# Four edits to a two-layer transformer kernel: loads of the FFN's first token rows, preset rows of a table, unread products in TensorE's waits, and the place of the last shared expert

## The chip, the cores and the metric

The kernel runs on one core of one Trainium2 chip, in fp32. The metric is the device time in microseconds of one execution. The kernel before takes 2078.44 us, the median of three runs (2077.82, 2078.44, 2081.33). TensorE is called PE, VectorE DVE, ScalarE ACT, GpSimd POOL and SyncE SP.

## The reference

The input `x` has 8 batches of 512 tokens with 256 channels. Four residual blocks follow one another; each normalises `x` first.

```python
x = x + _L0_attn_ref(_layernorm(x), ...)  # 16 heads, relative positions in 128 buckets, own layernorm
x = x + _L0_ffn_ref(_layernorm(x), ...)
x = x + _L1_attn_ref(_layernorm(x), ...)
x = x + _L1_ffn_ref(_layernorm(x), ...)
```

In the second block (shortened below) each batch has weights of its own: token rows 1 to 16 of the batch are split into even and odd ones, and their outer products are added to the common weights.

```python
lt = x[:, 1:17, :]; even = lt[:, ::2, :]; odd = lt[:, 1::2, :]
m1 = (even[:, :4, :, None] * odd[:, :4, None, :]).reshape(Bx, Hx, Dx)
m2 = (even[:, 4:, :, None] * odd[:, 4:, None, :]).reshape(Bx, Dx, Hx)
h = einsum('bsd,hd->bsh', x, W1) + scale * einsum('bsd,bhd->bsh', x, m1) + b1
out = einsum('bso', gelu(h), W2) + scale * einsum(gelu(h), m2) + b2
```

The third block is attention over the batch dimension, with a mask under which the first four batches see batches 0 to 3 only, and the last four see all eight. The fourth is a mixture of 32 experts. A token takes 4 of them, chosen out of its 2 best groups of 8 by sigmoid scores, and adds the output of a shared expert, which every token passes through.

## The kernel before

The first block (`_l0_attention`, from 0 to about 1081 us) runs over a list of attention steps. A dictionary (`prefetch`, L585 on) says which pieces of the next block's preparation are done how many steps before its end: at -12 the load of w1T, at -8, -6, -5 and -4 batch 0's statistics, its normalised tile `xn0` and its two transposes, and at the last step the load of w2T.

The second block (`_FFN`, 1082 to about 1325 us) runs over the 8 batches. For one batch, `hidden` (L676) makes 8 tiles of 128 hidden channels, each of two products 128x128 by 128x512 accumulated in PSUM tile `ph`; `output` (L684) makes four output tiles; `fold` (L641 for w1b, L646 for w2b) makes the next batch's own weights on DVE, eight operations on each. The even rows that `fold` multiplies must stand on all 128 partitions. `norm` writes 16 token rows to a small table in DRAM (L609), and `spread` (L614) loads 8 of them back into `even`, 128 partitions x 8 x 256, 1 MB in one DMA. For batch 0 that load is issued when the FFN begins; for the others it is issued at f = 2 of the batch before. All these DMAs are on SP's queue.

On that queue, too, `fill` (L693) writes zeros into one eighth of `rows`, the table of 160 x 128 rows in DRAM through which routed tokens reach their experts: at f = 2 of batches 0 to 6 for the first seven parts, and after the last output of batch 7 for the last one. The last call then writes a column of numbers from tile `spare` (L697, 20480 elements of 4 bytes).

The third block and the routing of the fourth (`_l1`, 1325 to about 1810 us) run over 8 units u of 512 tokens. Their order is written out by hand: `at(time, f)` puts a call on a list, `hop` puts a call in two halves on it, and the list is sorted by time and emitted in that order on all engines. Each unit's chain is `multiplied` (DVE, prod), `summed` (PE, ps, L972), `scored` (PE, pts, L988; ACT copies sc), `softmax1` and `softmax2` (DVE and ACT), then per seen batch `weighted` (DVE, value) and `gathered` (PE, ao, L1025, eight transposes accumulated in PSUM), and `projected` (PE, po). `prepare` transposes and projects a unit that comes two later (PE pq, pv; L935, L947). PSUM tiles come from the two-buffer pool `quick`, among others.

A unit is routed one unit later, interleaved with the next unit's attention: `norm2` (ACT, xn), `turn2` (PE, pt, L1088), `logits` (PE), `hidden` twice (PE pg and pu, ACT act; the shared expert's two halves, L1248), `route` (DVE, sfc to tmp to sel), `count`, `take` and `send` (PE pc, pb, pk and DVE between), `gated` twice (DVE, hid), `copied` four times (ACT, pay), `add_shared` (PE pos). Then POOL scatters the unit's 16 groups of rows to the table by indirect DMAs (L879). `pace` issues two of these at a time, and each pair waits for what DVE did last at that point. The last unit's routing stands alone, since no attention comes after it; this part is called the rear here.

`experts` reads off which expert owns each of the 160 tiles. Then the expert stage (1816 to 2090 us) fetches tile after tile of the table (r, L1414, on SP, each waiting for the last 16 scatters), transposes it (PE ptr, L1432; rT), multiplies (pge, L1440), transposes and multiplies again (pth, poe), and scatters results.

Of the kernel before, what the change touches and what calls it, by code (L numbers as in the profile page):

```python
# [21 lines left out]
P = 128  # L22
# [532 lines left out]
class _FFN:  # L555
# [30 lines left out]
    def prefetch(self):  # L586

        return {
            -200: [self.constants],
            -12: [self.load],  # L590
            -8: [partial(self.measure, 0)],
            -6: [partial(self.norm, 0)],
            -5: [partial(self.turn, 0, 0)],
            -4: [partial(self.turn, 0, 1)],
            0: [self.load2],
        }

# [5 lines left out]
    def norm(self, b, bank, pool):  # L603
        nc = self.nc
        xn = self.xn[b] = (pool if b else self.carry).tile([P, NT, H], F32, tag="xn" if b else "xn0", name="xn")
        for t in range(NT):
            _normalize(nc, xn[:, t, :], self.x[b][:, t, :], *self.stats[b], t)
            if t == 0:
                nc.sync.dma_start(self.token_rows[b % 2], xn[1:17, 0, :])  # L609

    def spread(self, b, pool):

        even = pool.tile([P, 8, H], F32, tag="even", name="even")
        self.nc.sync.dma_start(  # L614
            even, self.token_rows[b % 2].rearrange("(i two) c -> two i c", two=2)[0].partition_broadcast(P)
        )
        w1 = pool.tile([P, NK, FF], F32, tag="w1b", name="w1b")
        w2 = pool.tile([P, NF, H], F32, tag="w2b", name="w2b")
        self.w[b] = even, w1, w2
# [14 lines left out]
    def fold(self, b, n):  # L634

        nc = self.nc
        even, w1, w2 = self.w[b]
        for i in range(4):
            if n < 2:
                cols = slice(i * H, (i + 1) * H)  # L640
                nc.vector.scalar_tensor_tensor(  # L641
                    w1[:, n, cols], even[:, i, :], self.odd[:, n, i : i + 1], self.w1[:, n, cols], ALU.mult, ALU.add
                )
            else:
                view = lambda w: w.rearrange("p (r q) o -> p q r o", q=2)[:, n - 2, :, i * 64 : (i + 1) * 64]
                nc.vector.scalar_tensor_tensor(  # L646
                    view(w2),
                    even[:, 4 + i, :].rearrange("p (o r) -> p r o", r=4),
                    self.odd[:, n - 2, 4 + i : 5 + i],
                    view(self.w2),  # L650
                    ALU.mult,
                    ALU.add,
                )

    def run(self, rest, after):

        nc, tc, x, rows = self.nc, self.tc, self.x, self.rows
        with ExitStack() as ctx:
# [30 lines left out]
            def fill(n):  # L689

                part = slice(n * NS // B, (n + 1) * NS // B)
                to = rows.rearrange("(s p) c -> p s c", p=P)[:, part]
                filled.append(nc.sync.dma_start(to, empty.unsqueeze(1).to_broadcast([P, NS // B, ROW])))  # L693
                if n == B - 1:
                    with nc.allow_non_contiguous_dma(reason="a column of rows"):
                        filled.append(
                            nc.sync.dma_start(  # L697
                                rows.rearrange("(s p) c -> p s c", p=P)[:, :, H : H + 1].bitcast(I32), spare.unsqueeze(2)
                            )
                        )  # L700

            with tc.manual_schedule():
                self.spread(0, sb)
                nc.gpsimd.memset(empty, 0.0)
                nc.sync.dma_start(spare, self.a["spare"])
                for n in range(4):
                    self.fold(0, n)
                for b in range(B):
                    hT = sb.tile([P, NF, S], F32, tag="hT", name="hT")
                    for f in range(NF):  # L710
                        hidden(b, f)
                        if rest:
                            rest.pop(0)(bank, sb)
                        if f == 1:
                            for t in range(NT):
                                nc.gpsimd.tensor_tensor(x[b][:, t, :], x[b][:, t, :], self.b2, ALU.add)
                        if b == B - 1:
                            if f == 2:
                                after.measure(0)
                            elif f == 3:  # L720
                                after.shift(0)
                            elif f == 4:
                                after.norm(0)
                            continue
                        if f == 0:
                            self.measure(b + 1, bank, sb)
                        elif f == 2:
                            self.norm(b + 1, bank, sb)
                            self.spread(b + 1, sb)
                            fill(b)  # L730
                        elif f in (4, 5):
                            self.turn(b + 1, f - 4, bank, sb)
                    for t in range(NT):
                        output(b, t)
                        if b + 1 < B:
                            self.fold(b + 1, t)
                    if b == B - 1:
                        fill(b)
                    elif b == 2:
                        after.load()  # L740
        return filled

# [59 lines left out]
def _l1(nc, tc, a, x, out, ident, mhalf, rows, results, filled, inputs, early):  # L802
# [14 lines left out]
    with ExitStack() as ctx:  # L817
# [72 lines left out]

        waiting = deque()

        def pace():

            for _ in range(min(2, len(waiting))):
                after(waiting.popleft()(), [vec.last] if vec.last is not None else [])

        def quick(name):

            return ps_a.tile([P, S], F32, tag="psa", name=name)  # L900
# [401 lines left out]
        def at(time, f, *args):  # L1302
            events.append((time, len(events), partial(f, *args)))
# [26 lines left out]
        def attend(u, t):  # L1330
# [10 lines left out]
            )  # L1341
            at(t + when[0], softmax1, u)
            at(t + when[1], softmax2, u)
            for m in range(n):
                at(t + when[2][m], weighted, u, m)
                at(t + when[2][m] + 1.4, gathered, u, m)
# [3 lines left out]
        def routed(u, t, n):  # L1350

            at(t + 0.2, measure2, u)
            at(t + 5.0, norm2, u)
            at(t + 8.2, turn2, u)
            at(t + 10.0, logits, u)
            at(t + 13.4, hidden, u, 0)
            at(t + 20.0, hidden, u, 1)
            split = route(u)
            at(t + 15.3, next, split)
            at(t + (21.1 if n == 8 else 19.0), next, split, None)  # L1360
            late = 3.5 if n == 8 else 0.0
            hop(count, u, first=t + 23.4 + late / 2, then=t + 25.0 + late)
            at(t + (19.6 if n == 8 else 18.9), gated, u, 0)
            hop(take, u, first=t + 26.0 + late, then=t + 27.8 + late)
            at(t + 29.5 + late, gated, u, 1)
            for i in range(TOPK):
                at(t + 24.6 + late + 1.1 * i, copied, u, i)
            hop(send, u, first=t + 28.0 + late, then=t + 30.5 + late * 1.8)
            for r in range(2):
                hop(add_shared, u, r, first=t + 32.6 + late + r, then=t + 36.5 + late * 2 + 0.7 * r)  # L1370
            for i in range(8):
                at(t + 36.0 + late * 1.8 + 2.6 * i, pace)

        T = [40.0 if seen(u) == 4 else 48.0 for u in range(U)]
        start = [sum(T[:u]) for u in range(U + 1)]
        at(-29.0, biases)
# [22 lines left out]
        with tc.manual_schedule():  # L1399
            for _, _, f in events:  # L1400
                f()
            while waiting:
                pace()
            experts()
        routing.close()
        tp = pool("m_t", 2)
        ps_r = pool("m_psr", 2, space=PSUM)
# [277 lines left out]
```

## Time and profile before

| what | value |
|---|---|
| timed runs, median (lowest, highest) | 2078.44 us (2077.82, 2081.33) |
| the profiled execution, whole | 2102.91 us |
| its span | 2101.1 us |
| its mean granted TensorE clock | 0.954 |
| PE busy | 1930.6 us, 92% |
| PE weight loads (beside it) | 1334.9 us, 64% |
| DVE, ACT, POOL busy | 1389.0, 1106.3, 1143.3 us |
| chain that ended last | PE 63%, DVE 11%, DMA 11%, issue 5%, POOL 5%, ACT 3% |
| DMA moved | 444.43 MB, 212 GB/s mean |

By stage, PE is busy as follows, with the mean granted clock and the DMA engines' share:

| stretch, us | what | PE busy, us | clock | DMA |
|---|---|---|---|---|
| 1026 to 1082 | end of the first block | 49.37 of 56 | 0.94 | 0.75 |
| 1082 to 1325 | FFN | 234.34 of 243 | 0.99 | 0.60 |
| 1325 to 1794 | units and routing | 385.40 of 469 | 0.90 | 0.18 |
| 1794 to 1816.5 | wait for routed rows | 0.00 of 22.5 | 0.50 | 0.35 |
| 1816.5 to 2090 | experts | 268.39 of 273.5 | 0.99 | 0.73 |

The profile is of one execution, so durations are read from it and the times to compare from the runs. In a line of a timeline the columns are start, duration, engine, line of code, operation, output tile and inputs with their shapes, and the number of instructions put together; what stands in brackets at the end is how long the engine was idle before it and what ended that. A waits row gives engine and line, what it waited for, total us, number of waits and longest wait.

### The profile page before, as it was taken

Reading aid. Unit: us, or ns where it says so; the run is one execution under the profiler, and the core shown is the slowest. Engines: PE = TensorE matmul, PEld = TensorE weight load, DVE = VectorE, ACT = ScalarE, POOL = GpSimd, SP = SyncE. Lnnn points to the kernel's source line nnn. Section 1 sums busy time; section 2 is a strip of 40 time slices with the busy share of each in tenths; the row PEclk is TensorE's granted clock in tenths of the full one; section 3 lists DMA queues with packets and bytes.
Section 4 is the critical chain, followed back from the end, with each engine's and each line's share of the span. In section 5 each row is a group of like instructions: output and inputs, shape, how many; then the busy total and the mean of one; then the engine's idle time right before and its main releaser. Section 6 shows DMA issues by size and latency. Waiting matters only on the chain.

```text
span 2101.1 us, 49496 instructions
## 1 busy us (share of the span) xinstructions
PE 1930.6 (92%) x17956; PEld 1334.9 (64%) x17956; DVE 1389.0 (66%) x3731; ACT 1106.3 (53%) x2366; POOL 1143.3 (54%) x1340
## 2 busy tenths in 40 slices
PE   7999999999999999999889999879888778599997
PEld 4666667666666666676656666545455455388786
DVE  3677777777777777777676454257876775356666
ACT  2677777767777777677631222345433422144443
POOL 4666777767778686776733111114444443455555
PEclk7999999999999999999989999999989987699999
DMA  8999999999999999899944548601111115457888
GB/s 270 305 317 284 310 303 300 292 289 304 295 297 304 296 306 299 286 289 299 285 140 143 167 141 127 20 1 42 42 42 42 42 42 215 169 163 217 256 254 266
DMA packets 388928, 444.43 MB, mean 212 GB/s; under 512 B 43344, under 2 KB 367952, under 8 KB 388688
## 3 DMA queue, kind: packets, MB, share of 16 engines
q1 hardware_dynamic: 373904, 401.93, 63.9%
q0 software_dynamic: 13824, 38.29, 5.0%
q8 instruction: 145, 2.38, 0.5%
q10 hardware_dynamic: 960, 1.05, 0.1%
q14 instruction: 95, 0.78, 0.1%
HBM read 238.99 MB, written 202.19 MB: 210 GB/s over the span
## 4 chain that ended last, share of the span: by engine, by line
PE 63%; DVE 11%; DMA 11%; issue 5%; POOL 5%; ACT 3%; SPq 1%; another core or an unknown queue 0%; POOLq 0%; DVEq 0%; ACTq 0%
PE sc L372 7%; PE sc L384 6%; PE pge L1440 6%; PE et_ps L412 5%; PE po L684 5%; DMA winp<-shift 5%; PE ctx_ps L424 5%; PE pq L291 5%; PE ph L676 3%; PE poe L1458 3%; PE pa L315 3%; DMA shift<-strip 3%; PE pq L935 2%; PE po L460 2%; DVE prod L796 2%
## 5 line engine op out<-in xcount | busy, mean ns | idle before, releaser
L398 DVE CUSTOM_DVE_ANT_0 e<-sc,winc 128x512 f32<-128x512 f32 x512 | 333.3, 689 | 268.1 <-PE sc L384 139.4
L401 ACT ACTIVATE e<-e,low 128x512 f32<-128x512 f32 x512 | 365.7, 715 | 94.8 <-DVE low L398 93.5
L322 ACT COPY strip<-pa 128x512 f32<-128x512 f32 x512 | 275.2, 591 | 138.6 <-POOL winc L352 58.2
L325 POOL TENSOR_TENSOR own<-aside,strip 128x512 f32<-128x512 f32 x256 | 269.1, 1051 | 130.3 <-ACT strip L322 121.6
L415 DVE COPY et<-et_ps 128x512 f32<-128x512 f32 x512 | 328.5, 683 | 0.7 <-PE et_ps L412 0.7
L372 PE MATMUL sc<-sm,sm 32*128 32x256 f32 (+3 forms) x1792 | 310.5, 437 | 0.2
L315 PE MATMUL pa<-pos,sm 32*128 32x256 f32 x2048 | 297.2, 407 | 1.7 <-ACT sm L299 1.0
L879 POOL DMA_INDIRECT rows<-pay,slot x128 | 141.4, 1105 | 237.2 <-issue 224.9
L352 POOL TENSOR_TENSOR winp<-winp,own 128x256 f32<-128x256 f32 x256 | 187.3, 732 | 108.0 <-DMA winp<-shift 78.3
L372 PEld LDWEIGHTS sc<-sm,sm 32*128 32x128 f32 x1792 | 164.1, 184 | 97.0 <-DVE et L415 35.6
L384 PE MATMUL sc<-ident,winp 128*128 128x128 f32 x1280 | 204.9, 287 | 22.4 <-DMA winp<-shift 21.1
L879 POOL DMA_INDIRECT results<-y,r x160 | 157.0, 981 | 124.3 <-ACT y L1460 70.7
L352 POOL TENSOR_TENSOR winc<-winc,own 128x256 f32<-128x256 f32 x256 | 187.2, 731 | 52.2 <-DMA winc<-shift 40.6
L384 PEld LDWEIGHTS sc<-ident,winp 128*128 128x128 f32 x1280 | 137.4, 142 | 102.0 <-issue 58.3
L315 PEld LDWEIGHTS pa<-pos,sm 32*128 32x128 f32 x2048 | 178.5, 187 | 11.5 <-issue 2.0
L412 PE MATMUL et_ps<-ident,e 64*128 64x64 f32 x4096 | 184.2, 230 | 1.1 <-DVE et L415 1.1
L58 POOL TENSOR_TENSOR rstd<-var,mhalf 128x2 f32<-128x2 f32 (+1 forms) x56 | 51.1, 912 | 241.5 <-DVE var L56 208.9
L412 PEld LDWEIGHTS et_ps<-ident,e 64*128 64x128 f32 x4096 | 148.9, 140 | 44.4 <-issue 22.8
L1440 PE MATMUL pge<-store,rT 128*128 x640 | 168.0, 385 | 3.5 <-DVE rT L1434 1.1
L424 PE MATMUL ctx_ps<-et,v 128*32 128x128 f32 x4096 | 166.6, 281 | 0.5 <-DVE et L415 0.5
L291 PE MATMUL pq<-xnT,wqk 128*128 128x512 f32 x256 | 134.0, 646 | 0.1
L679 ACT ACTIVATE hT<-ph,b 128x512 f32<-128x512 f32 x64 | 44.0, 687 | 165.6 <-PE ph L676 165.5
(216 smaller groups left out, 3339.0 us busy)
## 6 DMA issues: line engine op xcount, KB each, us to landing
shift<-strip SPq DMA_DIRECT2D x256, 510.0 KB
winp<-shift SPq DMA_DIRECT2D x128, 384.0 KB
winc<-shift SPq DMA_DIRECT2D x128, 384.0 KB
winp<-shift SPq DMA_DIRECT2D x128, 256.0 KB
winc<-shift SPq DMA_DIRECT2D x128, 256.0 KB
rows<-empty SPq DMA_DIRECT2D x8, 2640.0 KB
r<-rows SPq DMA_DIRECT2D x160, 132.0 KB
z<-results SPq DMA_DIRECT2D x32, 512.0 KB
```

Of the source, the lines that this page charges most:

```text
L315: nc.tensor.matmul(pa[:, t * W : (t + 1) * W], src[rs, i * P : (i + 1) * P], pos[rs, g, :], start=True, stop=True)
L322: nc.scalar.copy(st[:, 2 * j : 2 * j + 2, :].rearrange("p t w -> p (t w)"), pas[j])
L352: nc.gpsimd.tensor_tensor(dst, dst, own[:, t], ALU.add)
L372: nc.tensor.matmul(sc[:, c0:c1], s[side_][rs, cut : cut + P], s[2 + side_][rs, c0:c1], start=c0 == 0, stop=False, skip_group_check=True,)
L384: nc.tensor.matmul(sc[:, m * P : (m + 1) * P], wins[n + 2 * (m - i)][1][:, j, (i - m + 1) * P : (i - m + 2) * P], ident, start=False, stop ...
L398: nc.vector.tensor_tensor_reduce(e, sc, wins[n][0][:, j, :], 1.0, -LOW, ALU.add, ALU.min, low)
L401: nc.scalar.activation(e, e, AF.Exp, bias=low, scale=-1.0, accum_out=totals[b, g // 2][:, i, r : r + 1])
L412: nc.tensor.transpose(bank[:, c : c + 64], e[rs, m * P : (m + 1) * P], ident[rs, rs])
L415: nc.vector.tensor_copy(et[:, f].rearrange("p j m q -> p (j m q)"), bank)
L424: nc.tensor.matmul(ctx_ps[32 * r : 32 * r + 32, i * P : (i + 1) * P], vs[b % 2][:, m, g % 2, g // 2 * 4 + r, :], et[:, :, m, :], start=m = ...
L879: ins = nc.gpsimd.indirect_dma_start(to, bass.IndirectOffsetOnAxis(ap=index, axis=0), source, None, bounds_check=last)
L1440: nc.tensor.matmul(pg[:, :H], rT[:, k * P : (k + 1) * P], w[:, k * H : (k + 1) * H], start=k == 0, stop=k == NK - 1)
```

## The change

There are four parts.

1. Batch 0's first four even rows are loaded at step -3 of the first block, into a tile that takes over a slot of the carried pool ("xn2"). For every batch the tile `even` becomes two tiles of half the size, loaded by one DMA each; `fold` of w1b reads the first, of w2b the second.
2. The last `fill` is called at f = 7 of the last batch but one, not after the last output; the column of numbers is written by a call of its own at f = 0 of the last batch.
3. `busy(n)` issues n products of 128x128 by 128x512 on weights that lie in SBUF, into a PSUM tile that nothing reads. They are put at times before the first `gathered` of units 0, 1, 4, 5, 6 and 7, before a `summed` or `gathered` of units 6 and 7, and at 8.19 after the beginning of the last routing; 14 more, in pairs, stand behind seven of the last 13 scatters, each pair waiting for one of them.
4. In the rear, the shared expert's second `hidden` and both `gated` come at 30.9 to 31.5, behind both halves of `send` (28.0 and 30.5), not at 18.9 to 29.5; the 16 scatters of the last unit no longer wait for DVE's last operation.

```diff
+            -3: [self.spread_first],
...
+    def even_rows(self, b, half, pool, tag):
+        even = pool.tile([P, 4, H], F32, tag=tag, name="even")
+        rows = self.token_rows[b % 2].rearrange("(i two) c -> two i c", two=2)[0]
+        self.nc.sync.dma_start(even, rows[4 * half : 4 * half + 4].partition_broadcast(P))
+        return even
+
+    def spread_first(self, *_):
+        self.first = self.even_rows(0, 0, self.carry, "xn2")
...
-        even = pool.tile([P, 8, H], F32, tag="even", name="even")
-        self.nc.sync.dma_start(
-            even, self.token_rows[b % 2].rearrange("(i two) c -> two i c", two=2)[0].partition_broadcast(P)
-        )
+        even = [self.even_rows(b, 0, pool, "even0") if b else self.first, self.even_rows(b, 1, pool, "even1")]
...
-                    w1[:, n, cols], even[:, i, :], self.odd[:, n, i : i + 1], self.w1[:, n, cols], ALU.mult, ALU.add
+                    w1[:, n, cols], even[0][:, i, :], self.odd[:, n, i : i + 1], self.w1[:, n, cols], ALU.mult, ALU.add
...
-                    even[:, 4 + i, :].rearrange("p (o r) -> p r o", r=4),
+                    even[1][:, i, :].rearrange("p (o r) -> p r o", r=4),
...
                         if b == B - 1:
-                            if f == 2:
+                            if f == 0:
+                                number()
+                            elif f == 2:
...
+                        elif f == 7 and b == B - 2:
+                            fill(b + 1)
...
-                    if b == B - 1:
-                        fill(b)
-                    elif b == 2:
+                    if b == 2:
...
-        def pace():
+        def pace(free=False):
             for _ in range(min(2, len(waiting))):
-                after(waiting.popleft()(), [vec.last] if vec.last is not None else [])
+                ins = waiting.popleft()()
+                if not free:
+                    after(ins, [vec.last])
+
+        def busy(n, behind=()):
+            idle = quick("idle")
+            for _ in range(n):
+                ins = nc.tensor.matmul(idle, inputs.wqkv[:, 0, :P], inputs.wqkv[:, 1, :S], start=True, stop=True)
+                if behind:
+                    after(ins, behind)
+                    behind = ()
...
+            if u in WAITS:
+                at(t + when[2][0] + 1.39, busy, WAITS[u])
+            if u >= U - 2:
+                at(t + 7.89, busy, 3)
...
+            if u + 1 == U:
+                at(t + 8.19, busy, 4)
...
-            at(t + 20.0, hidden, u, 1)
+            rear = u + 1 == U
+            at(t + (31.0 if rear else 20.0), hidden, u, 1)
...
-            at(t + (19.6 if n == 8 else 18.9), gated, u, 0)
+            at(t + (30.9 if rear else 19.6 if n == 8 else 18.9), gated, u, 0)
...
-            at(t + 29.5 + late, gated, u, 1)
+            at(t + (31.5 if rear else 29.5 + late), gated, u, 1)
...
-                at(t + 36.0 + late * 1.8 + 2.6 * i, pace)
+                at(t + 36.0 + late * 1.8 + 2.6 * i, pace, u + 1 == U)
+        WAITS = {0: 5, 1: 2, 4: 5, 5: 1, 6: 3, 7: 3}
...
             experts()
+            for ins in scattered["rows"][-13::2]:
+                busy(2, [ins])
```

More of the change, by code (lines that the diff above doesn't have):

```diff
@@ L693, in fill, with number @@
                 filled.append(nc.sync.dma_start(to, empty.unsqueeze(1).to_broadcast([P, NS // B, ROW])))
[L694 to L699, printed above, removed]
+            def number():
+                with nc.allow_non_contiguous_dma(reason="a column of rows"):
+                    filled.append(
+                        nc.sync.dma_start(
+                            rows.rearrange("(s p) c -> p s c", p=P)[:, :, H : H + 1].bitcast(I32), spare.unsqueeze(2)
                         )
+                    )
             with tc.manual_schedule():
```

## The prediction

> **What bounds the kernel.** I read the page's engine totals and its strip of slices first, then the chain, then TensorE's waits, then windows of 3.41 us. TensorE (PE) is busy 1930.6 of 2101.1 us and carries 63% of the chain, so the end moves with PE time or with what PE waits for.
>
> ```profile
> PE   7999999999999999999889999879888778599997
> PEclk7999999999999999999989999999989987699999
> ```
>
> Each digit of these rows is 52.5 us. After the first slice the granted clock is lowered in slice 20 (1051 to 1103 us, where the FFN begins) and in slices 29 and 32 to 34 (1523 to 1576 and 1681 to 1839 us, units 4 to 7 and the rear). Those stretches are where the change works. PE's waits from 1325 to 1830 us (total, count, longest) say why:
>
> ```profile
> PE ao L1025 <- DVE value L796: 32.2, 10, 7.1
> PE ptr L1432 <- DMA r<-rows: 23.1, 1, 23.1
> PE ps L972 <- DVE prod L796: 9.5, 7, 4.3
> ...
> PE pt L1088 <- ACT xn L1076: 5.4, 1, 5.4
> ```
>
> A wait is dear twice: itself, and at the clock behind it. The granted clock moves only on a grid of 3.41 us. Columns: stretch, its length, busy PE, PEld, DVE, ACT, POOL, granted clock, DMA share, GB/s.
>
> ```profile
> 1369.04:1372.46 3.42, 0.00 (x0) 0.00 (x0) 1.20 (x3) 2.09 (x3) 0.00 (x0) 0.50 0.01 2
> 1410.00:1413.41 3.41, 1.43 (x10) 1.19 (x11) 3.27 (x21) 0.90 (x2) 0.00 (x0) 1.00 0.01 2
> 1519.23:1522.64 3.41, 1.54 (x5) 0.47 (x4) 3.13 (x17) 3.33 (x5) 0.00 (x0) 1.00 0.00 0
> 1737.68:1741.09 3.41, 3.41 (x17) 3.01 (x15) 3.38 (x10) 0.00 (x0) 0.00 (x0) 0.50 0.00 0
> ```
>
> The reader sees the idle slot at half clock; a slot 42% busy that kept it (next slot full); one 45% busy after which it fell; and a slot filled wholly with transposes and narrow products that did not raise it. Over all slots, at most 0.40 busy always dropped and 0.48 or more never.
>
> **First rows of the FFN (5.2 us).** Before, the 1 MB of even rows is issued at 1081.92, when the FFN begins; folds start at 1087.64 and PE's first hidden product follows.
>
> ```profile
> 1087.64 3.26 DVE L641 SCALAR_TENSOR_TENSOR w1b<-even,odd,w 128x256 f32<-128x256 f32 x8 [5.00 <-DMA spare<-in_spare]
> ...
> 1088.23 3.75 PE L676 MATMUL ph<-xnT,w1b 128*128 128x512 f32 x4 [6.39 <-issue]
> ```
>
> Afterwards batch 0's first half lands three attention steps earlier. The fold starts at about 1081.9, the cn multiply (0.69) and seven folds of 0.41 follow, and PE's two k halves run at about 1082.4 and 1084.7. The first hidden tile is done at about 1085.5, not 1091.65: 6.1 earlier. But DVE, which still folds w2b (4.74) and then normalises batch 1, moves only from 1095.56 to about 1090.6, and batch 1's transposes queue on PE behind that normalising. I take 5.2; 4 if the second half, still issued at 1081.9, comes late to the w2b folds, 6.5 if DVE has slack. On SP the early half stands before the w2T load, which comes 0.5 to 1.5 us later and is wanted only at 1085.9: nothing. Every batch has two half loads in place of one, one SP issue of 0.41 us more each, in an SP queue whose wait is for DMA: nothing, at most 0.4 in all.
>
> **Last preset and number column (0).** In the instruction order of the built programs the last two fills, the numbers and the next loads stand on SP in the same order with equivalent waits as before. SP already runs ahead:
>
> ```profile
> 1277.42 7.94 SPq L693 DMA_DIRECT2D rows<-empty  x2
> 1299.70 0.36 SPq L697 DMA_DIRECT2D rows<-spare  x1
> ```
>
> The first line's start follows batch 7's token rows (written at 1275.60), the numbers follow the landing of the last fill, and ACT's first xlT copy, which waits until they land at about 1333.7, keeps PE waiting 6.8 us. All of it moves with the FFN and none of it with the new places: 0, and the FFN's 5.2 carries through.
>
> **Products in the waits.** One 128x128 by 128x512 product is half of a two-product tile: 0.86 us at full clock, 1.71 at half (pg, four products in 3.41 to 3.62 us). Their own waits are on ACT reads long finished; whatever is queued behind them on PE was waiting for DVE anyway. They cost nothing if they are shorter than the wait and save only what is now run slowly behind it.
>
> Unit 0: five products (4.27) in 7.08 us. The slow work behind, ao 1.97 instead of 1.09 and pq 5.08 instead of 3.44, is 2.5. A hole of 2.8 remains, which can straddle a grid line; I take half, 1.25 (0.8 to 2.5). Unit 1: no drop here, 0 (to 1.5 in other executions). Unit 4: five in 6.78 leave 2.5, at most 1.9 behind; 1.4. Unit 5: one product in 1.52, while the 4.25-us wait later (for tmp) stays: 0. Unit 6: three before ps 0.4, and three in front of the first ao:
>
> ```profile
> 1680.18 1.97 PE L1025 MATMUL ao<-ident,value 128*128 128x128 f32 x8 [4.21 <-DVE value L796]
> ...
> 1689.09 1.23 DVE L796 TENSOR_TENSOR value<-v,sc 128x1024 f32<-128x1024 f32 x1 [2.62 <-PE ao L1025]
> ```
>
> DVE there waits 2.62 for the slow ao's to free a value buffer; at full clock that wait goes: 2.6, with ps 3.0. Unit 7 has the same 4.21 and the same 2.62 at 1744.00: 2.6. Here the built order holds a surprise. The four products timed for the last routing's wait do not stand there: two join the three before unit 7's first ao (five, 4.27 in 4.21: +0.1), the others follow ao's. The 5.40-us wait before the last transposes stays empty, and its cold stretch (1761.58 to 1775.23) with it.
>
> A rule weighed here: the Trainium skill, "TensorE: Matmul & The Clock Gate", section "HAM oscillation — how this bites in real kernels", says that gaps over about 3.4 us throttle PE. By it the holes of 2.8 and 2.5 left in units 0 and 4 are safe and these units give 2.5 + 1.9 = 4.4. The trace differs: waits of 1.87 us (1520.20) and 2.25 (unit 6, pts) dropped the clock and 3.47 (1408.5) did not, since what counts is how full a grid slot is. I follow the trace: 2.65.
>
> **Last unit's shared expert behind its ranks (3.2 us).** DVE's route, the road to the scatters, now stands behind hid of half 0:
>
> ```profile
> 1776.13 0.69 DVE L796 TENSOR_TENSOR hid<-act,pu 128x512 f32<-128x512 f32 x1 [2.58 <-issue]
> 1776.76 0.27 DVE L796 TENSOR_TENSOR tmp<-sfc,rank 128x128 f32<-128x128 f32 x1
> ```
>
> Without it tmp starts at 1773.55 (1776.13 less 2.58), 3.2 earlier. Then come ranks, slots and scatters, first one at 1787.3 instead of 1790.49. What moves: on PE half 1's four products behind pk (3.41 cold), on ACT its act behind the four pay copies, on DVE both hids (0.69 each) behind the write of dest, then pos; all this runs until about 1800, hidden by the 16 scatters, whose last is at 1811.59 now. On POOL the scatters lose their wait for DVE's last operation (queued behind it: only further scatters), after which GpSimd alone paces them at about 1.28 us; a 2.2-us hole between the second and third (1791.46 to 1793.67), while 12.6 MB of expert weights still land, may go (+2.2) or may grow by the 3.2 gained, if that load is its cause. Hence 1 to 5.4; I take 3.2.
>
> **Products behind the scatters (2.8 us).** The 23.08-us wait for the first routed rows leaves PE cold until 1823.02:
>
> ```profile
> 1818.18 2.04 PE L1440 MATMUL pge<-store,rT 128*128 x4 [0.56 <-DMA r<-rows]
> ```
>
> Fourteen products in seven pairs, each pair waiting on every second of the last scatters (2.56 us apart, 1.71 of work, 67% of a slot), lift the clock before the rows come. The 6.5 us at half clock lose about 2.8 (1.5 to 3.1); the last pair ends about a microsecond before the rows, and if it is cold (3.41) delays them by 1.0.
>
> **Sum.** 5.2 + 0 + 1.25 + 1.4 + 3.0 + 2.6 + 3.2 + 2.8 = 19.4 (19.45). The profiled execution's span is 2101.1 (2102.91 with what lies around it), 1.2% above the timed median 2078.44. The pieces come from that slower execution: span 2081.7. Carried over unscaled to the median: 2059.0.
>
> **Rivals.**
> One, likeliest (0.53): as summed, 2059, own range 2055 to 2063.
> Two (0.18): the products do not hold the clock, since the holes left and the transposes behind (the 1737.68 slot) drop it anyway. Left are 5.2 + 3.2 + 2.8 = 11.2: 2067.
> Three (0.12): the clock holds everywhere, as the rule has it (4.4 for units 0 and 4), and the scatter hole goes too: 19.4 + 1.75 + 2.2 = 23.4, so 2055.
> Four (0.08): two, and the head start fails as well: on SP the early half stands behind the attention's last winp and winc loads (5% of the chain are such loads), and if it lands no sooner than 1086 the folds start where they did. Left are 3.2 + 2.8 = 6, at the low bounds 1 + 1.5: some 3, about 2075, within the measurement.
> Five (0.09), slower: the waits begin at half clock in timed executions. It decides at the point where a slot before the wait is under 0.4 full; unit 7's first ao is the place, five products taking 8.5 us in a 4.21-us wait. All 29 cold take 49.6 us against waits of 35.9: +13.7, less the 8.4 of FFN and rear: +5.3, so 2084.
>
> The change doing less than it says is in the sum: the moved fills and the four strays count nothing.
>
> **How the numbers follow.** About 0.2% (4.2 us) is what a measurement can tell from no change. Faster: one, two, three, 0.83; within: four, 0.08; slower: five, 0.09. The range reaches from 2050 (three with the upper bounds of FFN and rear) to 2070 (two with FFN at 4 and tail at 1.5), and leaves out four and five.
>
> **What would show it.** Right: first fold at about 1082 and FFN ending 5 us earlier; fills, numbers and ACT's wait earlier by the FFN's 5 us and no more; clock 1.00 behind unit 6's and 7's first ao and DVE's 2.62 gone; 5.4 before the last transposes still there; first scatter 3 us earlier relative to those transposes; pge under 1.1 at the first expert tile. Wrong: first fold at 1087 again (four), busy products of 1.7 us each with ao starting later than value (five), or clock 0.5 behind filled waits (two).

## The result, and the profile after

The kernel after takes 2060.67 us (median of 4 runs, 2052.38 to 2062.2), the one before 2079.89 in the same comparison. The ratio is 0.9905, 95% interval 0.9884 to 0.9926, that is 19.8 us less (15.4 to 24.1); the two medians differ by 19.2. The forecast was 2059.0. A second comparison gave 2070.39 against 2092.14 us, ratio 0.9901 (0.9878 to 0.9924). The profiled execution of after took 2052.38 us and has a span of 2050.6. That is 50.5 less than the profile before, more than twice what the runs show; so two single profiles must not simply be subtracted, and the table below takes two profiles of each.

The two strips of the page of after, to be laid beside those of before (40 slices of 51.3 us):

```profile
PE   7999999999999999999989999989888887899997
PEclk7999999999999999999999999999999998999998
```

The low clock in the slice where the FFN begins is gone, and of the four lowered ones behind it, up to the experts, one is left, slice 33 (1692 to 1743 us): unit 7 and the rear. PE's waits of after from 1000 to 1830 us (total, count, longest):

```profile
PE ao L1047 <- DVE value L807: 13.1, 8, 2.8
PE pc L1189 <- DVE past L807: 7.2, 3, 4.5
PE pu L1270 <- DVE hid L807: 5.6, 2, 4.0
PE pt L1110 <- ACT xn L1098: 5.4, 1, 5.4
...
PE ps L994 <- DVE prod L807: 4.7, 9, 1.7
...
PE ptr L1466 <- DMA r<-rows: 0.5, 1, 0.5
```

The 32.2 us before ao have become 13.1 and the 23.1 before ptr 0.5, filled with products. Not all of it was filled: the wait before pc is 7.2 us, 2.1 in the profile before (its longest there 1.1, now 4.5, in unit 6). The 5.4 before the last transposes stand as before. The first expert tile on PE begins warm:

```profile
1771.13 0.63 PE L1466 MATMUL ptr<-ident,r 128*128 128x128 f32 x4 [0.53 <-DMA r<-rows]
1772.70 1.10 PE L1474 MATMUL pge<-store,rT 128*128 x4 [0.93 <-DMA r<-rows]
```

Before, these were 1.09 and 2.04. The FFN's beginning on DVE:

```profile
1066.75 0.48 DVE L649 SCALAR_TENSOR_TENSOR w1b<-even,odd,w 128x256 f32<-128x256 f32 x1 [1.56 <-POOL empty L713]
1067.16 0.68 DVE L449 TENSOR_TENSOR cn<-cn,spread 128x512 f32<-128x512 f32 x1
1067.75 2.85 DVE L649 SCALAR_TENSOR_TENSOR w1b<-even,odd,w 128x256 f32<-128x256 f32 x7
1070.80 4.76 DVE L654 SCALAR_TENSOR_TENSOR w2b<-even,odd,w 128x256 f32<-128x256 f32 x8 [0.19 <-DMA even<-token_rows]
```

The fold starts ahead of cn, not 5.7 us behind it, and the second half is only 0.19 late. The rear's route, from its last transposes to the first of its 16 scatters:

```profile
1722.15 2.80 PE L1110 MATMUL pt<-ident,xn 128*128 128x128 f32 x8 [5.41 <-ACT xn L1098]
1732.34 0.29 DVE L807 TENSOR_TENSOR tmp<-sfc,rank 128x128 f32<-128x128 f32 x1
1744.94 0.98 POOL L890 DMA_INDIRECT rows<-pay,slot  x1 [10.96 <-issue]
```

The line tmp comes 10.19 us behind the transposes' start; before it was 13.75 (1776.76 less 1763.01). Stage lengths in us, each from the timelines; "first, second" are two profiled executions of the same kernel:

| stage | before: first, second | after: first, second | forecast gain |
|---|---|---|---|
| start to cn multiply (first block) | 1081.95, 1083.90 | 1067.16, 1074.45 | 0 |
| cn to batch 0's first xn addition on DVE | 13.51, 13.46 | 8.31, 8.27 | 5.2 |
| from there to the FFN's end (first bias product) | 230.17, 230.21 | 230.00, 230.02 | 0 |
| from there to the first pq (the wait for xlT) | 8.81, 8.34 | 2.34, 7.78 | 0 |
| unit 0, first ao to its projection | 13.41, 13.55 | 10.90, 10.89 | 1.25 |
| unit 3, unit 2's projection to its first ao | 42.47, 42.48 | 40.88, 40.87 | 0 |
| units 4 and 5, from projection to projection | 96.03, 93.90 | 94.26, 93.89 | 1.4 |
| unit 6, likewise | 58.93, 58.73 | 56.04, 56.04 | 3.0 |
| unit 7, likewise | 54.91, 53.70 | 51.42, 51.40 | 2.6 |
| rear, last transposes to first scatter | 27.48, 24.78 | 22.79, 24.22 | 3.2 |
| last scatter to first poe | 12.29, 12.08 | 9.95, 10.02 | 2.8 |
| first poe to the end | 277.22, 273.34 | 274.58, 273.11 | 0 |

The first block alone differs by 14.8 us between the first two profiles, and no part of the change runs there until its last steps. Another 6.5 of the 50.5 are the wait for xlT, which below is long in some jobs and short in another, whatever the kernel. A scatter is counted from its start in this table.

### The profile page after: what moved, and what is told of

Its sections match the earlier page's. It is cut to its first block, busy times and chain, and to the rows that moved or that the text cites. A ratio compares the mean times of both kernels' runs of the same rounds, so it can differ in the third digit from the quotient of the medians.

```text
span 2050.6 us, 49678 instructions
## 1 busy us (share of the span) xinstructions
PE 1937.0 (94%) x18042; PEld 1329.2 (65%) x18042; DVE 1390.9 (68%) x3731; ACT 1107.2 (54%) x2366; POOL 1142.1 (56%) x1340
## 5 line engine op out<-in xcount | busy, mean ns | idle before, releaser
L291 PE MATMUL pq<-xnT,wqk 128*128 128x512 f32 x256 | 129.1, 626 | 0.1
```

## The experiments

Each kernel ran on one of three chips together with the kernel before, and was profiled once. (The chips of the first two profiles are not on record.) Times are medians, ratios are to the kernel before of the same job. A ratio is the comparison's own estimate, not the quotient of the two medians: for the even rows below it says 10.0 us (5.4 to 14.6), where the medians differ by 5.6.

**The four parts alone.** The edits are the hunks of the diff: part 1; part 3 without the products behind the scatters; part 4; the products behind the scatters.

> Only the halved even rows with batch 0's first half loaded early (part 1); fills, products and rear as before. My theory (the parts add up): 5.2 us faster than before, about 2074 against 2079; from the cn multiply to batch 0's first xn addition on DVE 8.3 us instead of 13.5, and the FFN's end 5.2 nearer to the cn multiply. Rival (the head start is given back, or the extra half loads cost SP or DMA time): 0 to 1 us. In both, PE's wait for xlT after the FFN shows whether that wait belongs to the number column's new call, as the profile of after could suggest (6.8 before, 0.3 after): if the wait is there here, the new call may be its cure; if it is gone, it varies between executions.

> Only the 29 unread products within the units (part 3 without the 14 behind the scatters). My theory: the clock holds behind the filled waits, 8.25 us faster by the prediction's terms (1.25 + 1.4 + 3.0 + 2.6), 10.6 by the terms that the profile of after shows (2.5 + 1.3 + 0.5 + 2.9 + 3.4); clock full behind unit 6's and unit 7's first ao. Rival (the products do not hold the clock in most executions): 0 to 2 us faster. Rival (products run cold): slower.

> Only the last unit's shared expert behind its ranks and its scatters without the wait for DVE (part 4). My theory: 3.2 us faster by the prediction's term, 4.6 by the profile of after (3.56 at tmp and 1.1 at the ranks' products); the 2.2-us hole between the second and the third scatter stays, as in the profile of after. Rival (the moved products and hids delay the index or the expert stage): 0 or slower, with the expert stage's first transpose later than 5.1 us behind the last scatter.

> Only the 14 unread products behind the last scatters. My theory: 2.8 us faster by the prediction's term, 2.45 by the profile of after (first to fourth tile at full clock). Rival (the products delay the first routed rows' transposes, or the clock was warm anyway): 0 or up to 1 us slower.

| part alone | time, us (before 2086.93) | ratio (interval) | its stage, us |
|---|---|---|---|
| even rows | 2081.29 | 0.9952 (0.9930 to 0.9974) | cn to first xn addition 8.38 |
| products in the units | 2082.80 | 0.9969 (0.9949 to 0.9989) | unit 6 56.04, unit 7 51.40, unit 0 12.59 |
| rear | 2084.08 | 0.9982 (0.9966 to 0.9999) | transposes to first scatter 23.58 |
| products behind scatters | 2088.90 | 1.0007 (0.9986 to 1.0028) | last scatter to first poe 12.92 |

The product of the four ratios, with that of part 2 below, is 0.9907, the ratio of the whole. But each is known to about 0.002, so the product to some 0.004 or 9 us, and the differences of the medians add up to 11.1 us only. So the times agree with parts that add up and do not prove it; the stages must. In their own stages the first three do what the theory says. In the others they differ from the kernel before by little more than its own profiles differ; the exception is the rear alone, with 50.63 us for unit 7, where it has no product (see unit 7 below), and 10.97 from the last scatter to the first poe. The last is a miss, as to the time and in its stage: there the first routed rows landed 7.10 us behind the last scatter, where the other profiles of that job have 5.05 to 5.10, and after a 2.58-us hole PE was cold again.

```profile
1800.44 1.96 PE L904 MATMUL idle<-wqkv 128*128 128x512 f32 x4 [0.61 <-DMA rows<-pay,slot]
1804.97 0.99 PE L1445 MATMUL ptr<-ident,r 128*128 128x128 f32 x4 [2.58 <-DMA r<-rows]
1806.45 2.04 PE L1453 MATMUL pge<-store,rT 128*128 x4 [0.50 <-DMA r<-rows]
```

The last pair ended at 1802.4 and did not delay ptr; a DMA did. With transposes in these places (below) the rows came 6.3 us behind the last scatter, with products and the moved rear together 5.07 to 5.24 in five profiles. Why they were late here, no run shows.

**The same kernels once more, and part 2 alone.** The profile of after has a wait of 0.33 us for xlT where all five others until then had 4.25 to 6.81, so part 2, put at nothing, might be worth 4 to 8.

```diff
-                if n == B - 1:
-                    with nc.allow_non_contiguous_dma(reason="a column of rows"):
...
+            def number():
...
+                            if f == 0:
+                                number()
...
+                        elif f == 7 and b == B - 2:
+                            fill(b + 1)
```

> The kernel before, once more, for a second profile of it. If the differences between the first two profiles that no part of the change touches (15 us in the first block, 1.6 us at unit 3, up to 2 us in the expert stage) vary between executions, they move here by like amounts; PE's wait for the first xlT should be 4.2 to 6.8 us, as in every profile so far of a kernel without part 2.

> The kernel after, once more. If the 0.33-us wait for the first xlT in its first profile comes from part 2, it is under 1 us here; if it was chance, 4 to 5 us. By my theory the time is 19 us under before's on the same chip. Unit 6's first value to its projection 16.0 us as before, unit 0's 10.9 or 12.6 by where the clock's grid falls.

> Only the last preset and the number column at their new places (part 2); the order of SP's queue is the one of before. By the prediction: nothing, the wait for the first xlT stays at 4.2 to 6.8 us. Rival, from the profile of after: the column lands earlier, the wait is under 1 us, and the kernel is 4 us faster, 6 where the clock fell behind it.

Before again: 2093.21 us, 0.9999 (0.9982 to 1.0016). Part 2 alone: 2091.68 us, 0.9997 (0.9979 to 1.0014). The first pq in the second profile of after, and in that of part 2 alone:

```profile
1320.52 2.90 PE L957 MATMUL pq<-xlT,wqkv 128*128 128x512 f32 x3 [5.77 <-ACT xlT L948]
```

```profile
1343.14 3.75 PE L938 MATMUL pq<-xlT,wqkv 128*128 128x512 f32 x4 [5.68 <-ACT xlT L929]
```

The wait is there with part 2. On this chip the rival falls, and the forecast of nothing for part 2 holds. The four profiles of this job, all on one chip, have 5.68 to 6.34 us whatever the kernel; the four of the first job, on a second chip, 4.25 to 4.75.

**The number column's tile kept.** The new tile xlT takes the place of the column's source tile, which the DMA still reads. The experiment puts that tile into the carried pool:

```diff
-            spare = wp.tile([P, NS], I32, tag="spare", name="spare")
+            spare = self.carry.tile([P, NS], I32, tag="spare", name="spare")
```

> After, with the number column's source tile in the carried pool, so that no later tile takes its place and ACT's first xlT copy need not wait until the column has landed. If that wait is what holds PE for 4 to 6.8 us in eight of nine profiles, it is under 1 us here, the clock does not fall behind it, and the kernel is 4 to 8 us faster than after. Rival (the wait is for something else that lands as late, or its time comes back later in unit 0): the same time as after.

It took 2071.34 us against 2081.47, ratio 0.9956 (0.9934 to 0.9977). The wait was 0.33 us; but two kernels of the same job, on a third chip, that did not keep the tile had 0.33 and 0.47. On that chip the DMA share falls to nothing some 25 us after the column's issue and the first pq starts 28.5 to 28.8 us after it; on the other two pq starts 32.4 to 34.4 us after it. So there was no wait to take away, and whether this edit pays on the other two chips was not tried. Every kernel profiled on the third chip has part 2, so that it is the chip that makes the wait short there, and not part 2 on that chip, is likely but not shown.

This job also shows less gain than the first two comparisons. The interval of this kernel (0.9934 to 0.9977) does not meet those of after (0.9884 to 0.9926 and 0.9878 to 0.9924), though it has the whole change: 9.2 us, not 19.8 or 20.7. The job's other three kernels, below, gain 7.3 to 15.6 us by their ratios. By stages this one lacks 1.7 us against after in unit 0 and 2.2 to 3.6 in the rear. After itself was not in this job, and no profile of the kernel before was taken in it, so whether the change is worth less on this chip is open.

**Products moved and added.** The first two lines are put at the head of norm2; joined lists the projections' additions on DVE. Against after:

```diff
+            if u + 1 == U:
+                busy(4, [joined[-1]])
...
-            if u + 1 == U:
-                at(t + 8.19, busy, 4)
+            if u in (5, 6):
+                at(t + 23.39 + late / 2, busy, 2)
...
-        WAITS = {0: 5, 1: 2, 4: 5, 5: 1, 6: 3, 7: 3}
+        WAITS = {0: 7, 1: 3, 4: 7, 5: 1, 6: 4, 7: 4}
```

> After, with the products moved and added: four stand before the last unit's transposes, held there by a wait for the last addition of its projection; two more before the count of units 6's and 7's time, four before their first ao, seven before unit 0's and 4's, three before unit 1's. My theory (what counts is how full each 3.41-us slot is): the rear's transposes, logits and first hidden half run at full clock, from those transposes to the first scatter 20.5 us instead of 22.8; unit 7's first ao no later than value; unit 0 10.9; about 4 us faster than after. Rival (transposes let the clock fall anyway, and the extra products run cold): the rear as in after and unit 7's ao later by 1.7 per added product.

> The kernel of the moved and added products, with the number column's source tile carried too. If both edits are worth what their stages showed (1.3 at unit 7, up to 1 in the rear, 4 to 8 at the wait for xlT), it is 5 to 9 us faster than after and the fastest kernel of the study; if the moved products are worth nothing, as their time so far says, the same as with the carried tile alone.

The first took 2072.12 us, 0.9897 (0.9874 to 0.9919), beside 0.9901 for after on the same chip: no difference that this comparison can tell. By stages it is a mixed answer. Unit 0 took 10.90 in both kernels: seven products leave a hole of 1.09 us where five leave 2.80. (Both profiles of after have 10.90 too, by chance, as said under unit 0 below.) Unit 7 took 50.14 instead of 51.40. Unit 6 gained nothing, 56.07. The rear is the instructive one:

```profile
1742.64 3.70 PE L915 MATMUL idle<-wqkv 128*128 128x512 f32 x8 [0.92 <-DVE x L807]
1747.13 0.33 PE L1112 MATMUL pt<-ident,xn 128*128 128x128 f32 x1 [0.79 <-ACT xn L1100]
...
1748.61 0.98 PE L1112 MATMUL pt<-ident,xn 128*128 128x128 f32 x5 [0.16 <-ACT xn L1100]
1749.61 3.84 PE L1120 MATMUL pl<-rw,xT 128*128 128x32 f32 x16
```

The four products stand where they were meant to, and the transposes run at full speed; but the clock falls at 1749.02, behind a slot that was 62% busy (2.13 of 3.41 us), and the logits run cold (3.84 for 16, as 0.64 and 3.20 in after). From the transposes to the scores' first use it is 6.67 instead of 7.02 us. The second kernel, with the tile kept as well, took 2067.32 us, 0.9925 (0.9898 to 0.9951): the fastest median of its job, but its interval overlaps those of the others, and after itself was not in that job. No version tried is shown to be faster than after.

**Transposes in place of products.** Each unread product becomes three unread transposes of 128x128:

```diff
-                ins = nc.tensor.matmul(idle, inputs.wqkv[:, 0, :P], inputs.wqkv[:, 1, :S], start=True, stop=True)
+                for i in range(3):
+                    turn = nc.tensor.transpose(idle[:, i * P : (i + 1) * P], inputs.wqkv[:, 0, i * P : (i + 1) * P], ident)
+                    ins = ins if i else turn
```

> After, with each unread 128x512 product replaced by three unread 128x128 transposes of about the same length (0.82 us for 0.86). If any work in a slot holds the clock (a slot's fill is what counts, whatever fills it), unit 0, 6 and 7 run as in after: unit 0's first ao to its projection 10.9 us, unit 6's 16.0, unit 7's 15.5. If only wide products hold it, as the slot of the prediction suggests that was full of transposes at half clock, they run as in before: 13.4, 18.7 and 18.7, and the kernel is 7 to 10 us slower than after.

It took 2073.99 us, 0.9965 (0.9944 to 0.9987). By time this is not told apart from the other kernels of its job; by stages it is plain. Unit 6's first ao with transposes ahead of it, and then in after with products:

```profile
1646.94 2.18 PE L916 MATMUL idle<-ident,wqkv 128*128 128x128 f32 x9
1651.20 1.97 PE L1049 MATMUL ao<-ident,value 128*128 128x128 f32 x8 [2.08 <-DVE value L807]
...
1653.40 1.97 PE L1049 MATMUL ao<-ident,value 128*128 128x128 f32 x8
```

```profile
1641.26 4.36 PE L915 MATMUL idle<-wqkv 128*128 128x512 f32 x6
1645.50 1.09 PE L1047 MATMUL ao<-ident,value 128*128 128x128 f32 x8
...
1647.44 1.09 PE L1047 MATMUL ao<-ident,value 128*128 128x128 f32 x8
```

In unit 6 ao runs at half speed behind the transposes, as in the kernel before. From its first ao to its projection it is 18.75 us (before 18.74, after 16.04), in unit 7 18.57 (before 18.73, after 15.53). But the fillers were not of equal length, as the expectation took them to be (0.82 us for 0.86). In unit 0's wait fifteen transposes took 1.80 us at full clock, five products 4.46. So the experiment changed the amount of filler together with its kind. In unit 6 the clock was down when either filler began: the transposes took 2.18 us and left 2.08 open, the products took 4.36 and filled the wait. Unit 7 speaks against the kind as the cause:

```profile
1701.81 2.79 PE L916 MATMUL idle<-ident,wqkv 128*128 128x128 f32 x21
1706.12 1.09 PE L1049 MATMUL ao<-ident,value 128*128 128x128 f32 x8 [1.53 <-DVE value L807]
...
1708.14 1.97 PE L1049 MATMUL ao<-ident,value 128*128 128x128 f32 x8
```

The slot that held most of these transposes (1700.97 to 1704.38, PE busy 78%) kept the clock, and the first ao ran at full speed. The clock fell at 1707.79, behind a slot 38% busy, with the 1.53 us that the short filler left open. The Trainium skill ("TensorE: Matmul & The Clock Gate", section "🔬 Part 4: PE-mode transpose") says that a transpose does not count as PE-busy in the same way; the 78% slot, in which all but 0.2 us of PE's work was transposes, does not bear that out. A filler of transposes as long as the products was not tried. So the rival that any work holds the clock, if there is enough of it, stands.

What this run does show is that unread work in these places brings nothing by its mere presence. The gain follows DVE's wait for a value buffer, 2.62 us in units 6 and 7 of the kernel before. With transposes it is there again (2.62 and 2.45), and after has none in either unit. Its line at that place in unit 6 has no brackets, since DVE did not wait:

```profile
1650.59 2.34 DVE L807 TENSOR_TENSOR value<-v,sc 128x1024 f32<-128x1024 f32 x2
```

**After without the products behind the scatters.**

```diff
-            for ins in scattered["rows"][-13::2]:
-                busy(2, [ins])
```

> After, without the 14 products behind the last scatters. My theory: PE is cold when the first routed rows land, from their first transpose to the first poe 6 to 7 us instead of 4.8, and the kernel is 2 us slower than after. Rival, from the run that had these products alone (no gain): the same time within 1 us.

```profile
1780.82 1.09 PE L1464 MATMUL ptr<-ident,r 128*128 128x128 f32 x4 [16.32 <-DMA r<-rows]
1782.51 2.04 PE L1472 MATMUL pge<-store,rT 128*128 x4 [0.61 <-DMA r<-rows]
```

From the last scatter to the first poe it is 11.80 us, where the five profiles that have both the rear and these wide products have 9.90 to 10.12. From the first transpose to the first poe it is 6.70 us, in those five 4.76 to 5.05. The stage says 1.9; the time does not confirm it. It is 2068.08 us, ratio 0.9945 (0.9922 to 0.9967), which is less and not more than the 2071.34 of the kernel with the kept tile, and cannot tell 2 us. With the miss above, no comparison of times shows a gain from these products; it rests on the stage.

## Why the prediction was right, and where its terms were off

The sum was 19.4, the two comparisons show 19.8 and 20.7, with intervals of some 4.5 to each side. In the main the mechanism was right: the early rows let DVE go on earlier, a full clock behind the waits ends DVE's wait for PE, and the rear's route is shorter without the two hids. Unit 6 came out right by another way than the one forecast. That the sum meets the measured number within half a microsecond is partly luck: one by one the terms give less. The terms are checked with the mean of the profiles with and without the part in question (us; for the units those with the products as in after, not moved and not turned into transposes):

| term | forecast | without | with | shown |
|---|---|---|---|---|
| first rows of the FFN | 5.2 | 13.37 (6 profiles) | 8.25 (8) | 5.1 |
| fills and number column | 0 | ratio 0.9997 (0.9979 to 1.0014) | | 0 |
| unit 0, five products | 1.25 | 13.46 (6) | 11.89 (5) | 1.6 |
| units 4 and 5 | 1.4 | 94.56 (6) | 94.06 (5) | 0.5 |
| unit 6 | 3.0 | 58.82 (6) | 56.45 (5) | 2.4 |
| unit 7 | 2.6 | 53.27 (6) | 51.24 (5) | 2.0 |
| rear | 3.2 | 26.06 (6) | 23.53 (3) | 2.5 |
| behind the scatters | 2.8 | 11.93 (7) | 10.00 (5, with the rear) | 1.9 |

These sum to 16.0, within both intervals but at their lower end. Unit 3 adds 0.9 by the same reckoning, where no product was put; two of the six profiles without products have its shorter form too, so that this is where the clock's grid happens to fall and not a step of the change. What the last 3 us are, if they are any, the noise of the runs does not let one say. The range's lower end, 2050, was set lower than its terms give: 23.4 and the 1.3 that the FFN could add make 24.7, so about 2054.

**FFN.** Right in size and in reason: DVE and not PE's head start of 6.1 set it. The early half was there in time, so rival four is out; the stage from the first xn addition to the FFN's end stayed at 230.0.

**Fills and number column.** Right on the chip where it was tried alone, against what the first profile of after suggested. What I had not seen is that the wait behind them varies from job to job, probably by chip.

**Unit 0.** Right in kind. In two of the five profiles the 2.8-us hole let the clock be (10.9), in three it fell (12.5 to 12.6), about half, as taken. The rule on gaps over about 3.4 us that the prediction quotes from the Trainium skill ("TensorE: Matmul & The Clock Gate", section "HAM oscillation — how this bites in real kernels") would make this hole safe always, and it is not. Where the hole lay across two slots, which stayed 65% and 53% busy (first profile of after), the clock stayed; where it lay in one, 37% busy with the products alone and 18% with the kept tile, the clock fell.

Yet no one fill divides slots that keep the clock from slots that drop it. The prediction's "at most 0.40 busy always dropped and 0.48 or more never" holds for the units of its own profile, not for all its slots: in the first block of the same profile slots 51% and 58% busy (from 85.63 and 877.52) dropped it. So did one of 62% in the moved kernel (above) and one of 53% in unit 6 (below). What else counts, these runs do not show.

**Units 4 and 5.** Mis-sized. Unit 4 did run shorter by up to 1.7 (17.80 for 19.48 from its first ao to its projection, second profiles), but unit 5 then took 22.43 for 20.74. The step "at most 1.9 behind; 1.4" priced PE's time in unit 4 alone and did not ask what unit 5 waits for: from projection to projection both second profiles have 93.9.

**Unit 6.** Right in size, but only in part by the way forecast. The prediction put three products of 2.56 us in all into a wait of 4.21, to hold the clock. In four of the five profiles there was no clock to hold: an almost idle slot ahead of pc had dropped it (PE waits 4.1 to 4.5 us there), the three ran mostly at half clock, took 4.4 to 4.5 us, filled the wait, and so raised it again just before ao. In the fifth (after without the products behind the scatters) the clock was up:

```profile
1646.07 2.84 PE L915 MATMUL idle<-wqkv 128*128 128x512 f32 x6
1650.36 1.09 PE L1047 MATMUL ao<-ident,value 128*128 128x128 f32 x8 [1.45 <-DVE value L807]
```

The same three took 2.84 us and left 1.45 open, the clock fell at 1652.80, DVE waited 1.91 us, and the unit took 58.07 us, not 56.04 to 56.06. So three products are too few when they run warm; this luck is in the 2.4.

**Unit 7.** The step "five, 4.27 in 4.21: +0.1" failed in four of the five profiles, and it is rival five's mechanism at rival five's place. The slots of after there (stretch, length, busy PE, PEld, DVE, ACT, POOL, clock, DMA share, GB/s), and its PE timeline:

```profile
1688.72:1692.14 3.42, 1.48 (x6) 0.62 (x5) 3.04 (x22) 3.38 (x5) 0.00 (x0) 1.00 0.01 5
1692.14:1695.55 3.41, 3.41 (x5) 1.35 (x4) 3.31 (x5) 3.41 (x5) 0.00 (x0) 0.50 0.00 0
```

```profile
1691.18 0.22 PE L1189 MATMUL pc<-ones,past 128*32 128x1 f32 x2 [1.95 <-DVE past L807]
1691.34 6.25 PE L915 MATMUL idle<-wqkv 128*128 128x512 f32 x10
1697.43 1.04 PE L1047 MATMUL ao<-ident,value 128*128 128x128 f32 x8
```

PE waits 1.95 for pc just ahead, the slot is 43% busy, the clock falls, and the five products take 6.25. That puts ao about 1.9 behind its value. The 2.62 that DVE waited, and the slow ao's behind, paid for it: still 2.0 net. With two products ahead of pc and four behind it (the two kernels with moved products) four take 3.70 and unit 7 is 1.1 to 1.3 shorter. The clock's grid can do as much by itself: in the fifth profile the five ran warm, took 4.56, and the unit 50.34 us; with the rear alone, where no product stands, the clock came back in time for the third ao, DVE waited 0.44 us and not 2.62, and the unit took 50.63. That one is in the mean "without"; the other five there have 52.8 to 54.9.

**Rear.** Right in kind: tmp 10.18 to 10.19 us behind the transposes in the two profiles of after, 12.16 and 13.75 before. What is left to chance is whether the clock is up at pk: the ranks' read of it comes 1.75 us behind its start if it is, 2.5 to 3.1 if not. The 2.2-us hole at the scatters lies between the first and the second one, not the second and the third as the prediction has it. It was the same in every profile, with the wait for DVE and without, so it is not that wait. Nor did it grow when the scatters came 3 us earlier; but the experts' weights were landing beside it every time (DMA share 1.02 to 1.04), so that they cause it is not excluded. In the last job a stall of about 2.3 us on DVE's short operations stood in the route of all four kernels (26 us to the first scatter); its cause stays open. All four have the moved rear, and no kernel without it was profiled in that job. They are left out of the 23.53; with the two of them that have the products as in after it would be 24.7, and the rear worth 1.3.

**Behind the scatters.** Right in kind, 1.9 for 2.8 by the stage and not seen in the time: PE starts at full clock in every profile that has the wide products, but for the one in which the rows landed late. Five of the seven profiles "without" lack the moved rear as well; the two that have it took 10.97 and 11.80, so that 1.4 is the fairer figure.

**Rivals.** Two (the clock is not held, 11.2 us) is out by units 6 and 7, where ao runs at full clock, and by the intervals of both comparisons. Three (held everywhere, 23.4) lies within these and is out by units 0 and 7 and the unfilled rear. Five (products begin at half clock) happened in units 6 and 7 of most profiles: in unit 6 it filled the wait, in unit 7 it cost and was outweighed.

## What to carry to other kernels

Filler products pay where a wait is followed by PE work that another engine waits for: units 6 and 7 and, by its stage, the first expert tiles, and not unit 4, whose gain the next stage's wait took back. Count the fill of the slot before the wait too, since fillers that begin cold are themselves up to twice as long: three took 4.4 us cold and filled unit 6's wait, 2.8 warm and left a hole in which the clock fell. And measure a filler's length in its place: three transposes taken for one product were two fifths of it. When single profiles differ by 50 us and runs by 20, cut both into stages and profile each kernel twice before believing a stage.

## What the runs showed of the hardware

- The number column, 20480 writes of 4 bytes, let the work behind it begin 28.5 to 28.8 us after its issue on one chip and 32.4 to 34.4 on two others, one job on each; PE's wait there was 0.3 to 0.5 us, and 4.3 to 4.8 or 5.7 to 6.3.
- Unread products of 128x128 by 128x512 took 0.89 us each at full clock (five in 4.46), three mostly at half clock 4.36 to 4.54. Fifteen transposes of 128x128 took 1.80 us at full clock, nine 2.18 at half.
- Slots of 3.41 us that were 51, 53, 58 and 62% busy dropped the clock; slots 42 and 53% busy kept it, as did one 78% busy that held almost nothing but transposes.
- The kernel before had medians of 2079.9, 2086.9, 2092.1 and 2081.5 us in four jobs; ratios within a job (0.9905 and 0.9901) agreed far better than times.
